# First row group of a four-way recurrent convolution: rows placed within SBUF, x on two queues, first weights placed by PE, coefficient chain in PSUM

## The chip, the cores and the metric

The kernel runs on one core of one Trainium2 chip. The metric is the device time of one launch in microseconds (us). Everything is float32. In the profile PE is the matrix engine, PEld its weight loads, DVE the vector engine, ACT the scalar engine, POOL the GpSimd engine, and SP the engine that does nothing but issue DMAs; ACT and POOL issue some too. L741 is line 741 of the kernel before.

## The reference

The input x has 32 images of 48 channels, 64 rows (H) and 128 columns (W). Two layers each do x = x + conv(gn(x)); every layer has its own weights.

```python
def _gn(v, G=16, eps=1e-5):            # mean and variance per image and group of 3 channels
    g = v.reshape(B_, G, C_ // G, H_, W_)
    return ((g - mean(g)) / sqrt(var(g) + eps)).reshape(v.shape)

def step(w, b):                        # one step of a scan over rows or columns
    def f(carry, inp):
        nxt = inp + _conv1d(carry, w, b)     # 48 to 48 channels, 5 taps, along the other axis
        return (nxt, nxt)
    return f
# conv: scan down over the 64 rows, up again (same weights), right over the 128 columns, left again
x = x + _L0_conv_ref(_gn(x), ...)
x = x + _L1_conv_ref(_gn(x), ...)
```

Each scan is a chain: a row needs the row before it. All rows of an image must be read before its mean and variance, hence the scale and offset of its first row, are known.

## The kernel before, in words

The images form four groups of 8. `PHASES` lists twelve phases: a "rows" phase does the down and up scans of one group (2 x 63 steps), a "cols" phase the right and left scans of two groups (2 x 127 steps). Phase 0 is rows of group 0 in layer 0; phase 1 is rows of group 1. A step is 9 products on PE of 128x128 float32 (18 matmuls in the trace, L741) into three PSUM tiles, and three adds on DVE (L750) that put bias and input row on top. The step's matmuls of the next row wait for these adds.

For the products, a row lies as 384 values (8 column residues e = w mod 8, times 48 channels) over 3 blocks of 128 partitions (`PIECES`, ten runs of partitions, says where each (e, channel range) lies), and 16 column blocks x 8 images in the free dimension. Three slots of the SBUF tile `arena` hold half an image group's rows each; a fourth part of it is `stage`. The order of the work is written by hand: `at(t, fn)` puts a piece of work ahead of step t, and `in_order` fixes, engine by engine, the order in which the program gives the instructions. An engine that waits therefore holds back everything behind it.

What precedes phase 0 is `first_group`:

- x of group 0 comes by 16 DMAs on SP (`take_in`, one per image and half), with channel and half of the rows interleaved over 96 partitions. `parts[i]` holds one half. DVE takes statistics of each image (`bn_stats`, L422).
- The weights of the first scan go from DRAM to a DRAM scratch (`taps`), and from there by 25 small DMAs to their places; ten more bring the biases. All of these are on ACT's queue.
- Rows 0 to 7 come into step layout by products with 0/1 matrices on PE (`rows_by_product`, L1074) and copies from PSUM on ACT (L1081).
- All 64 rows are permuted by copies of POOL and ACT (`permute`, L569, four copies of 96x256 for a pair of rows) and written to DRAM (`put_out`, tensor `xin`); rows 8 to 63 come back from there in step layout (`move_rows`, ten DMAs for eight rows, in runs of 128 bytes). The copy in DRAM also serves the residual, later.
- `scaling` turns statistics into scale and offset: products with a mask on PE average over channel groups, and DVE and ACT form 1/sqrt(var + eps) with one Newton step (L354 to L401).
- The rows are scaled in place: rows 0 to 3 by DVE (`scale_at_once`, L625), rows 4 to 47 by ACT (`scale_rows`, L614), rows 48 to 63 by POOL (`scale_at_once` again).

Group 1's input is prepared during phase 0 by `plan_input`: loads into `nats1` (which lies where the second half of group 0's x lay), permuting on POOL, `put_out`, statistics on ACT (L443, L435), and `scaling` on DVE between the steps (L460, L465, L470 and on).

Of the kernel before, what the change touches and what calls it, by code (L numbers as in the profile page):

```python
# [120 lines left out]
def kernel(  # L121
# [49 lines left out]
    early = const([FULL, 3 * WEIGHTS + NG * N + BN], "early")  # L171
# [5 lines left out]
    wt["left"] = const([FULL, NG, NG * FULL], "wleft")  # L177
# [7 lines left out]
    junk = early[:, 3 * WEIGHTS + NG * N :]  # L185
# [34 lines left out]
    def lines(t, h0, h1):  # L220

        t = t.rearrange("c (i q a n) -> a c i q n", i=E8, q=NQ, a=NH)[h0 // E8]
        return t[:, h0 % E8 : h0 % E8 + h1 - h0].rearrange("c i q n -> c (i q) n")
# [53 lines left out]
    def sided(t):  # L277

        return t.rearrange("(c s) n -> s c n", s=2)

    def load_constants(dma):
        for s in range(2):
            dma(sided(mask_sb)[s], mask[SIDES[s], SIDES[0]])
        for e, c0, c1, o, p0 in PIECES:
            dma(bd[p0 : p0 + c1 - c0, o], bias[c0:c1])
# [5 lines left out]
    def spread_masks():  # L291
        for s in range(2):
            nc.gpsimd.tensor_copy(mask_x.rearrange("p (c s) -> p s c", s=2)[:, s], mask_sb)
        for e, c0, c1, o, p0 in PIECES:
            nc.gpsimd.tensor_copy(maskp[:, o, p0 : p0 + c1 - c0], mask_sb[:, c0:c1])

    def spread_row_masks():
        for s in range(2):
            nc.gpsimd.tensor_scalar(
                mask_r.rearrange("p o (c s) -> p o s c", s=2)[:, :, s],  # L300
# [10 lines left out]
    def scaling(key, layer, g, averages, masks, slack=0):  # L311
# [5 lines left out]
        pool = nc.gpsimd if slack else nc.vector  # L317
# [25 lines left out]
        mean = small("mean")  # L343
        spare = small("dev")
        dev = spare[0 : FULL if n > 1 else PX, 0:n]
        if n > 1:
# [3 lines left out]
            expand(ps[:, 1 : 1 + NG], mean_c)  # L350
            yield
            nc.vector.tensor_tensor(dev, mean_p, ps[:, 1 : 1 + NG], ALU.subtract)
        else:
            nc.vector.tensor_tensor(dev, mean_p, ps[0:PX, 0:1], ALU.subtract)  # L354
        if n > 1:
            nc.vector.tensor_copy(mean, ps[:, 1 : 1 + NG])
# [6 lines left out]
        if n == 1:  # L363
            expand(ps[:, 2 + NG :], dev[:, 0])
        else:
# [5 lines left out]
            expand(ps[:, 2 + NG :], var_c)  # L371
        yield
        var = small("var")
        nc.vector.tensor_scalar(var, ps[:, 2 + NG :], GN_EPS, None, ALU.add)

        std = small("std")
        nc.scalar.activation(std, var, AF.Sqrt)
        if n == 1:
            expand(ps[:, 1 : 1 + NG], mean_p[:, 0])
        yield  # L380
        if n == 1:
            nc.vector.tensor_copy(mean, ps[:, 1 : 1 + NG])
        yield
        for _ in range(slack):
# [4 lines left out]
        pool.tensor_tensor(t0, var, r0, ALU.mult)  # L389
# [3 lines left out]
        scale, offset = (  # L393
            stat_pool.tile(
                [FULL, NG, GB], F32, tag=f"{t}{layer}{g}", name=f"{t}{layer}{g}"
            )
            for t in ("scale", "offset")
        )
        pool.tensor_tensor(scale, r0, t0, ALU.mult)
        pool.tensor_tensor(offset, mean, scale, ALU.mult)  # L400
        pool.tensor_scalar(offset, offset, -1.0, None, ALU.mult)  # L401
        coeffs[layer, g] = scale, offset
# [150 lines left out]
    def take_in(g, r0, nat, batches=slice(0, GB)):  # L553


        n = nat.shape[-1] // W
        src = x[g * GB : (g + 1) * GB].rearrange("b c (s h) w -> (c s) b (h w)", s=2)
        dma(nat[:, batches], src[:, batches, r0 * W : (r0 + n) * W])
# [12 lines left out]
    def put_out(g, r, perm):  # L571


        n = perm.shape[-1] // (W * GB)
        for s in range(2):
            h = s * HALF + r
            dma(
                lines(source[0][g], h, h + n),
                sided(perm)[s].rearrange("p (m n) -> p m n", n=LINE),
            )  # L580
# [37 lines left out]
    def scale_at_once(k, h0, h1, eng):  # L618

        _, layer, g = PHASES[k]  # L620
        view = row_views(k)[h0 // HALF][:, :, h0 % HALF : h0 % HALF + h1 - h0]
        view = view.rearrange("p o h (k b) -> p o (h k) b", b=GB)
        for t, op in zip(coeffs[layer, g], (ALU.mult, ALU.add)):
# [585 lines left out]
```

## Time and profile before

| what | value |
|---|---|
| runs shown, median (lowest to highest) | 4286.53 us (4279.23 to 4295.52), 3 runs |
| profiled execution: time / span | 4290.3 us / 4288.2 us |
| PE busy, share of the span | 4058.9 us, 95% |
| DVE / ACT / POOL busy | 2164.5 / 1340.1 / 886.2 us |
| mean granted PE clock | 0.981 |
| DMA | 680.12 MB in 2116733 packets, 2005440 of them under 512 bytes |

The page gives busy times of the engines, and a map of the span in 40 slices. A timeline row reads: start in us, length in us, engine, line, operation, output tile <- input tiles, shapes, count, and in brackets the idle time before it and what ended it. A row of the waits reads: who waited for whom, us in total, times, longest. A row of windows gives for each engine the busy time and the number of instructions, then the granted clock, the busy share of the 16 DMA engines and GB/s. An answer on a tile gives for a kind of instruction the least, median and greatest duration in ns; for a DMA that is the time of its issue.

### The profile page before, as it was taken

Reading aid. Unit: us, or ns where it says so; the run is one execution under the profiler, and the core shown is the slowest. Engines: PE = TensorE matmul, PEld = TensorE weight load, DVE = VectorE, ACT = ScalarE, POOL = GpSimd, SP = SyncE. Lnnn points to the kernel's source line nnn. Section 1 sums busy time; section 2 is a strip of 40 time slices with the busy share of each in tenths; the row PEclk is TensorE's granted clock in tenths of the full one; section 3 lists DMA queues with packets and bytes.
Section 4 is the critical chain, followed back from the end, with each engine's and each line's share of the span. In section 5 each row is a group of like instructions: output and inputs, shape, how many; then the busy total and the mean of one; then the engine's idle time right before and its main releaser. Section 6 shows DMA issues by size and latency. Waiting matters only on the chain. (4 is left out here: it accounts for less than half of the span.)

```text
span 4288.2 us, 89979 instructions
## 1 busy us (share of the span) xinstructions
PE 4058.9 (95%) x36648; PEld 4029.3 (94%) x36648; DVE 2164.5 (50%) x6503; ACT 1340.1 (31%) x2662; POOL 886.2 (21%) x906
## 2 busy tenths in 40 slices
PE   3699998999999999998999999999999999999992
PEld 1699998999999999998999999999999999999992
DVE  6345444446664444444446654444444444444443
ACT  1584301435793564100006772613000002210122
POOL 4271001325323020010005310000000024510352
PEclk9899999999999999999999999999999999999996
DMA  9599799857998979679308979939289049999999
GB/s 213 113 216 162 105 167 168 245 127 213 230 198 156 163 140 160 103 127 206 85 1 242 222 154 149 148 50 161 43 140 200 1 78 247 247 243 156 180 202 182
DMA packets 2116733, 680.12 MB, mean 159 GB/s; under 512 B 2005440, under 2 KB 2056160, under 8 KB 2076384
## 3 DMA queue, kind: packets, MB, share of 16 engines
q1 hardware_dynamic: 2015904, 581.64, 70.2%
q10 hardware_dynamic: 97216, 86.44, 9.9%
q0 software_dynamic: 3200, 6.30, 0.5%
q8 instruction: 288, 4.72, 0.5%
q14 instruction: 125, 1.02, 0.1%
HBM read 397.38 MB, written 295.98 MB: 162 GB/s over the span
## 5 line engine op out<-in xcount | busy, mean ns | idle before, releaser
L614 ACT ACTIVATE arena<-arena,offset,scale 128x256 f32<-128x256 f32 (+2 forms) x816 | 575.6, 801 | 432.9 <-DMA arena<-mid 176.1
L673 POOL TENSOR_TENSOR arena<-arena 128x2048 f32<-128x2048 f32 x80 | 363.1, 4553 | 1386.0 <-PE step_10l L741 434.1
L569 POOL COPY arena<-arena 96x256 f32<-96x256 f32 x448 | 265.0, 650 | 553.8 <-DMA arena<-in_x 444.2
L512 ACT ACTIVATE early<-arena 128x256 f32<-128x256 f32 x192 | 129.4, 674 | 477.2 <-POOL arena L673 471.2
L741 PE MATMUL step_00r<-arena,early 128*128 128x128 f32 x2286 | 251.5, 274 | 14.1 <-DMA arena<-upa 14.1
L741 PEld LDWEIGHTS step_00r<-arena,early 128*128 128x128 f32 x2286 | 251.1, 185 | 14.5 <-issue 14.4
L741 PE MATMUL step_01r<-arena,early 128*128 128x128 f32 x2286 | 250.6, 273 | 14.4 <-DMA arena<-upa 14.4
L741 PEld LDWEIGHTS step_01r<-arena,early 128*128 128x128 f32 x2286 | 250.4, 185 | 14.6 <-issue 14.5
L741 PE MATMUL step_11r<-arena,early 128*128 128x128 f32 x2286 | 251.3, 273 | 8.2 <-DVE arena L750 8.2
L741 PEld LDWEIGHTS step_11r<-arena,early 128*128 128x128 f32 x2286 | 250.8, 185 | 8.7 <-DVE arena L750 8.6
L741 PE MATMUL step_00l<-arena,wleft 128*128 128x128 f32 x2286 | 249.1, 272 | 0.0
L741 PEld LDWEIGHTS step_00l<-arena,wleft 128*128 128x128 f32 x2286 | 248.6, 184 | 0.0
L741 PE MATMUL step_10l<-arena,wleft 128*128 128x128 f32 x2286 | 248.5, 272 | 0.0
L741 PE MATMUL step_11l<-arena,wleft 128*128 128x128 f32 x2286 | 248.5, 272 | 0.0
L741 PE MATMUL step_01l<-arena,wleft 128*128 128x128 f32 x2286 | 248.4, 272 | 0.0
L741 PE MATMUL step_10r<-arena,early 128*128 128x128 f32 x2286 | 248.4, 272 | 0.0
L741 PEld LDWEIGHTS step_10l<-arena,wleft 128*128 128x128 f32 x2286 | 248.4, 184 | 0.0
L741 PEld LDWEIGHTS step_11l<-arena,wleft 128*128 128x128 f32 x2286 | 248.4, 184 | 0.0
L741 PEld LDWEIGHTS step_01l<-arena,wleft 128*128 128x128 f32 x2286 | 248.4, 184 | 0.0
L741 PEld LDWEIGHTS step_10r<-arena,early 128*128 128x128 f32 x2286 | 248.4, 184 | 0.0
L698 ACT COPY arena<-arena 128x256 f32<-128x256 f32 x172 | 99.7, 656 | 411.5 <-POOL arena L673 162.2
L240 ACT COPY early<-arena 128x1 f32<-128x1 f32 x2 | 0.4, 191 | 657.9 <-DVE arena L750 657.9
(189 smaller groups left out, 7171.3 us busy)
## 6 DMA issues: line engine op xcount, KB each, us to landing
arena<-in_x SPq DMA_DIRECT2D x24, 1536.0 KB, 11.6
xin<-arena SPq DMA_DIRECT2D x96, 384.0 KB, 4.7
arena<-xin SPq DMA_DIRECT2D x96, 384.0 KB, 8.5
mid<-arena SPq DMA_DIRECT2D x96, 384.0 KB, 7.8
arena<-mid SPq DMA_DIRECT2D x192, 192.0 KB, 4.2
upb<-arena SPq DMA_DIRECT2D x192, 192.0 KB, 3.9
arena<-upb SPq DMA_DIRECT2D x96, 384.0 KB, 12.3
arena<-xin SPq DMA_DIRECT2D x186, 192.0 KB, 4.3
```

The source lines that it names most:

```text
L240: fn(*args)
L512: nc.scalar.activation(junk[:, 0:n], view[:, b], AF.Identity, accum_out=self.sum[:, i, j : j + 1])
L569: copy(dst[:, r, q], src[:, r0 + r, q])
L614: nc.scalar.activation(args[0], args[0], AF.Identity, bias=args[2], scale=args[1])
L673: eng.tensor_tensor(unit, unit, nat, ALU.add)
L698: copy(by_w(perm)[:, a], src[:, a])
L741: nc.tensor.matmul(part(whole(ps[o])[0:m], -s), weights[:, i, at : at + m], part(src(i), s), start=seen[o] == 1, stop=seen[o] == left[o],)
```

## The change

Layout: the two row sides of an image now lie in partitions 0 to 47 and 48 to 95 (before they alternated), so a load or store of both sides is two DMAs where it was one. The `left` weights join the tile `early`, where three weights' places lie free at first and serve as a ring buffer for four row copies.

First group: x comes in pairs of images, one side on POOL's queue and the other on ACT's. `parts[0]` now holds rows 0 to 31, `parts[1]` rows 32 to 63. Weights, biases and masks are loaded compactly on SP and placed by products of PE with 0/1 matrices, copied out by ACT. ACT's table for sqrt is loaded first. `four` copies four rows of each side into a buffer (a row as one copy of 96x1024) and 20 DMAs on SP place them from there straight into the step layout, in runs of 512 bytes; three buffers are used (`spot`, `ring`, `room`). `spot` lies where images 6 and 7 of `parts[1]` go, so these are loaded after it was read. The copies for DRAM (`to_cols`) follow apart, on POOL. Rows 0 to 3 are scaled by 24 operations of DVE (`scale_first`), all others by ACT.

Coefficients: in the chain without slack (groups 0, 1 and 3) intermediate values stay in PSUM, so no DVE operation has two operands in SBUF. Group 1's preparation is put 6 steps later, and its loads 22.

```diff
@@ scaling
+        if not slack:
+            far = ps[0:PX, 1 + NG : 2 + NG]
+            nc.vector.tensor_tensor(far, mean_p, ps[0:PX, 0:1], ALU.subtract)
+            nc.vector.tensor_tensor(dev, mean_p, ps[0:PX, 0:1], ALU.subtract)
+            nc.vector.tensor_tensor(far, far, dev, ALU.mult)
+            nc.vector.tensor_tensor(dev, far, var_p, ALU.add)
+            yield
+            expand(var, dev[:, 0])
+            yield
+            nc.vector.tensor_scalar(var, var, GN_EPS, None, ALU.add)
+            r0 = small("std")
+            nc.scalar.activation(r0, var, AF.Sqrt)
+            expand(mean, mean_p[:, 0])
+            yield
+            yield
+            nc.vector.reciprocal(r0, r0)
+            nc.vector.tensor_tensor(var, var, r0, ALU.mult)
+            nc.vector.tensor_tensor(var, var, r0, ALU.mult)
+            nc.vector.tensor_scalar(var, var, -0.5, 1.5, ALU.mult, ALU.add)
+            nc.vector.tensor_tensor(scale, var, r0, ALU.mult)
+            nc.vector.tensor_tensor(offset, mean, scale, ALU.mult)
+            nc.vector.tensor_scalar(offset, offset, -1.0, None, ALU.mult)
+            return
...
@@ take_in
-        src = x[g * GB : (g + 1) * GB].rearrange("b c (s h) w -> (c s) b (h w)", s=2)
-        dma(nat[:, batches], src[:, batches, r0 * W : (r0 + n) * W])
+        src = x[g * GB : (g + 1) * GB].rearrange("b c (s h) w -> s c b (h w)", s=2)
+        for s in range(2):
+            dma(nat[s * C : (s + 1) * C], src[s, :, :, r0 * W : (r0 + n) * W])
...
-    plan_input(1, [starts[0] + 46 + 6 * j for j in range(8)], 5, 1, nats1, tiles[2:4])
+    plan_input(1, [starts[0] + 52 + 6 * j for j in range(8)], 5, 1, nats1, tiles[2:4])
...
@@ first_group
+        ring = early[:, WEIGHTS : WEIGHTS + 4 * n]
+        spot = arena[:, 3 * SLOT + 2 * UNIT :]
+        room = arena[:, 2 * SLOT : 2 * SLOT + 4 * n]
...
+        def load(i, b0, b1, *sides):
+            for s in sides:
+                queue = nc.scalar if s else nc.gpsimd
+                dma(parts[i][s * C : (s + 1) * C, b0:b1], src[i, s, :, b0:b1], queue)
...
+        def place_rows(i, r0, n, perm):
+            src = perm[0:PX].rearrange("(s c) (r e m) -> s e c r m", s=2, r=n, e=E8)
+            dst = row_views(0)[i].rearrange("p o (s h) m -> s o p h m", s=2)
+            for s in range(2):
+                for e, c0, c1, o, p0 in PIECES:
+                    dma(dst[s, o, p0 : p0 + c1 - c0, r0 : r0 + n], src[s, e, c0:c1])
...
+        load(0, 0, 2, 0, 1)
+        load_kernel()
+        load_masks()
+        nc.vector.memset(junk[:, 0:1], 0.0)
+        nc.scalar.activation(junk[:, 0:1], junk[:, 0:1], AF.Sqrt)
+        make_select()
+        for b in range(2, 8, 2):
+            load(0, b, b + 2, 0, 1)
+        load(1, 0, 2, 0, 1)
+        load(1, 2, 4, 0)
+        load(1, 4, 6, 0)
+        place_kernel()
+        spread_masks()
         for b in range(GB):
             stats.take(0, parts[0], b)
...
+        pool, act = nc.gpsimd, nc.scalar
+        four(0, 0, spot, pool, pool, act, act)
+        to_four(0, 4, ring, pool, pool, act, act)
+        load(1, 2, 4, 1)
+        place_rows(0, 4, 4, ring)
+        load(1, 4, 6, 1)
+        load(1, 6, 7, 0, 1)
+        load(1, 7, 8, 0, 1)
+        four(0, 8, ring, pool, pool, act, act)
+        four(0, 12, ring, pool, pool, pool, pool)
         for b in range(GB):
             stats.take(NBN // 2, parts[1], b)
             stats.aggregate(b)
...
         for _ in scaling("x0", 0, 0, stats, x_masks):
             pass
...
+        scale_first(0, 4)
         scale_rows(0, 4, 8)
...
+        for h in range(8, HALF, 8):
+            scale_rows(0, h, h + 8)
+        blocks = [ring[:, j * n : (j + 1) * n] for j in range(4)]
+        for r in range(rows):
+            to_cols(0, r, blocks[r % 4])
+        for r in range(0, rows, 4):
+            four(1, r, (room, ring)[r // 4 % 2], pool, pool, pool, pool)
+        scale_rows(0, 32, 36)
+        scale_rows(0, 36, 40)
+        for h in range(40, H, 8):
+            scale_rows(0, h, h + 8)
+        for r in range(rows):
+            to_cols(1, r, blocks[r % 4])
         take_in(1, 0, nats1[0])
...
     for j in range(1, 4):
-        at(starts[0] + 22 + j, take_in, 1, 4 * j, nats1[j])
-    at(starts[0] + 26, scale_at_once, 0, 48, 56, nc.gpsimd)
-    at(starts[0] + 33, scale_at_once, 0, 56, 64, nc.gpsimd)
+        at(starts[0] + 44 + j, take_in, 1, 4 * j, nats1[j])
```

## The prediction

> **What bounds the kernel now.** I read the page first: PE is busy for 4058.9 of the 4288.2 us of the span, so what this change can move is time in which PE stands. The waits of PE over the first 260 us show where it stands early, and the timeline of PE shows when.
>
> ```profile
> PE rows L1074 <- DMA arena<-in_x: 41.7, 1, 41.7
> PE step_00d L741 <- DVE arena L750: 31.7, 6, 14.9
> PE step_00d L741 <- DVE arena L625: 24.7, 1, 24.7
> ```
> ```profile
> 107.83 17.66 PE L741 MATMUL step_00d<-arena,early 128*128 128x128 f32 x144 [24.72 <-DVE arena L625]
> ...
> 175.60 0.79 PE L741 MATMUL step_00d<-arena,early 128*128 128x128 f32 x2 [13.62 <-DVE arena L750]
> ...
> 208.63 0.80 PE L741 MATMUL step_00d<-arena,early 128*128 128x128 f32 x2 [14.85 <-DVE arena L750]
> 209.60 63.38 PE L741 MATMUL step_00d<-arena,early 128*128 128x128 f32 x556 [0.17 <-DVE arena L750]
> 272.81 73.28 PE L741 MATMUL step_00u<-arena,early 128*128 128x128 f32 x666
> ```
>
> The first scan starts at 107.83, stands three times (2.5, 13.6 and 14.9 us, at rows 8, 24 and 32, whose scaled values are not there), and turns upward at 272.81. A step is 18 matmuls; 666 in 73.28 us make 1.98 us a step. Sixty-three steps without a stand need 125 us, so 272.8 - 125 = 148 us is all that lies ahead of the turn besides PE's work.
>
> The timelines of DVE and POOL tell why the start is so late:
>
> ```profile
> 78.61 0.16 DVE L354 TENSOR_TENSOR dev_x<-mv_x_x,ps_x 96x8 f32<-96x8 f32 x1 [9.43 <-PE ps_x L322]
> ...
> 83.58 22.07 DVE L389 TENSOR_TENSOR dev_x<-var_x,std_x 128x24 f32<-128x24 f32 x1
> 105.68 0.18 DVE L390 TENSOR_TENSOR dev_x<-dev_x,std_x 128x24 f32<-128x24 f32 x1
> ```
> ```profile
> 100.96 4.64 POOL L569 COPY early<-arena 96x256 f32<-96x256 f32 x8
> ```
>
> A 0.18 us operation took 22.07 us and ended 0.05 us after POOL's row of copies (100.96 + 4.64 = 105.60). Before it, 9.43 us went in waiting for PE, which was still moving rows with its products.
>
> How x arrives and what an issue costs is in the windows and in SP's answer on the arena:
>
> ```profile
> 5.00:30.00 25.00, 0.00 (x0) 0.00 (x0) 12.34 (x20) 0.00 (x0) 0.00 (x0) 1.00 0.66 162
> 42.50:62.50 20.00, 20.00 (x23) 6.82 (x22) 17.92 (x32) 7.07 (x14) 9.21 (x25) 1.00 1.02 259
> ```
> ```profile
> L231 SPq DMA_DIRECT2D xin<-arena x26: 554/568/691, 44.7 to 91.7; - x26
> L231 SPq DMA_DIRECT2D arena<-xin x20: 312/823/1457, 74.1 to 103.2; - x20
> L231 SPq DMA_DIRECT2D arena<-in_x x16: 312/412/836, 0.7 to 42.2; - x16
> ```
>
> The last two numbers of a window are the DMA share and GB/s: 162 GB/s while the weights' small loads are mixed in, 259 GB/s with the 16 engines full.
>
> **The change, part by part.** *Coefficients.* L389 has its first operand in PSUM now: its 22.07 us go. So do the 9.43 us behind PE's products, which are dropped. The 24 scalings that `scale_first` adds on DVE I price at the 0.19 us of small DVE operations: 4.6 us; the upper bound is that they wait as L389 did, which is a rival below. The Trainium skill (SBUF — State Buffer, "Who interferes with whom") says that a DVE instruction with two SBUF inputs contends with GpSimd reads, as in L389's row, but also that tensor_scalar can enter a two-port mode and contend; by that rule the 24 would be held up to POOL's next pause.
>
> *Weights by PE.* The 25 placing DMAs and 10 bias DMAs (ACT's queue until 36.6 us) become 6 loads on SP and 38 matmuls. Bounds per matmul: 0.24 us (128x8) and 0.93 us (18 of 512 columns in 16.71 us), so 9 to 35 us; the pieces are mostly under 200 columns, so some 11 us from about 10 us on. That ends at 21, ahead of the rows on ACT, which come after the copies of the result: nothing. At the upper bound ACT's first rows would be 18 us late.
>
> *x on two queues.* x is 12.6 MB: 49 us at 259 GB/s. The first image took 5.6 us for 3.0 us of transfer, so 2.6 us of overhead, and part 0 (6.3 MB) lands at 24.3 + 2.6 = 27 us, not 44. One queue alone reached these 259 GB/s, so what two queues gain here is only the time that stalled issues cost up to 40 us. Against the second queue stands the Trainium skill, DMA: Bandwidth & Descriptors ("Rules for kernel authors"): spreading DMAs over issuing engines brings no bandwidth, as they share the same 16 engines; by that rule part 0 would land no sooner than at full rate, the same 27 us.
>
> *Rows SBUF to SBUF.* This is the new path. Before, 56 rows came back from DRAM in 128-byte runs and 8 by PE's products. Now all 64 are copied in 32 pairs by POOL and ACT, and each four copies (a set) are placed by 20 DMAs on SP. A shape between the rows above costs 0.41 to 0.57 us to issue; I take 0.50, so 10 us for a set, plus 2.5 to land. For 512-byte runs the engines stay below that: 1024-byte runs moved at 378 GB/s (43 ns on one engine), 128-byte runs at 158 GB/s (13 ns); 240 runs on each engine are 3 to 10 us. A row copy: 4 of 593 ns were 2.37 us; a 48-element one took 161 ns, so one of 1024 is about 2.2 us. POOL then also copies all 32 row pairs for DRAM, 16 copies = 38 us for each half.
>
> Order on the queues, each step from the one before:
> - 27: part 0 is in. 32: rows 0 to 3 copied.
> - 55: set 0 landed. Small transfers beside x wait their turn (a 36 KB one took 5.2 us beside x, a 192 KB one 3.1 us alone), so I add x's next six images (4.7 MB, 18 us) and the set's 10 us rather than overlap them.
> - The last two images lie where set 0's copies stand, so they are requested only now, from ACT and POOL, and land at 64; set 1 lands at 71. Sets 2 and 3 reuse one buffer, so POOL and ACT wait for landings; ACT's sqrt stands behind its two copies of set 2.
> - 76: copies of set 2, then sqrt. 78: coefficients. 83: first step, 25 us earlier than 107.83.
> - 88: set 2 landed; 97: set 3 copied on POOL; 109: landed; 12.3 us of scaling (24 of 128x128 on ACT): 122. Row 8 was due at 99, so PE stands 23 us.
> - 147: POOL's 38 us of copies for DRAM, which must finish before rows 32 on may overwrite part 0. 156: next set copied, 168 landed, 178 scaled; row 32 was due at 169: 9 us.
> - The last three sets are bound by SP and buffers: 178, 190, 200. Scaling rows 40 to 47 ends at 212, and row 63 at 212 + 23 x 1.98 = 258: the turn is 14 us earlier. (Row 40 was due at 194, so that stand is 18 us.) After a long stand the granted clock fell, to 0.50 in the window 200 to 210, and 32 matmuls came in the next 5 us in place of 48, so 1.7 us are lost; before has two such stands, the forecast three, which I leave within the rounding.
>
> *Group 1 gives most of that back.* Its loads need part 1 consumed: 200 + 38 = 238. The first landed 10 us after issue (225.3 to 235.3), so ACT's statistics start at 248 and need the 104.5 us they took (235.29 to 339.8): 352. DVE's first operation on the second pass (L470) came at 344.4 and phase 1's first matmul at 400.8, 56.4 later; the schedule now puts this 6 steps (11.9 us) later, leaving 44.5. So phase 1 starts no sooner than 352 + 44.5 = 397 against 400.8. DVE waits there in order, with the steps' adds behind it, so PE stands for about 10 us.
>
> The sum: -4 us. The profiled execution took 4290.3 us (span 4288.2), 3.8 over the median of 4286.5; 4290.3 - 4 - 3.8 = 4282.5, say 4283. Later groups' loads split in two halves cost one more issue (0.4 to 0.6 us) each on SP, in phases where PE does not wait for them; if that cover were gone, 24 x 0.5 = 12 us. The other edits only move buffers.
>
> **Rivals.** *Faster, the sets cost less.* At 0.41 us an issue eight sets on the path save 8 x 20 x 0.09 = 14 us, copies at 1.7 us another 7, set 0 hidden beside x up to 10: 31 us less, 4252. For it: 0.41 is a measured row. Against: that row has one run for each partition. If the sets were off the path altogether, the turn would come at 83 + 125 = 208: 4218; but POOL's 58 copies and the buffer reuse speak against it.
>
> *Slower, SP's queue.* The rows that SP wrote into the same pieces of partitions took 0.823 us (median). At that price the eight sets cost 8 x 20 x 0.32 = 51 us more: 4334. It decides from about 0.65 us an issue (25 us more). For it: the same ten pieces; against: those had 1536 runs of 128 bytes, these 192.
>
> *The wait is not removed but moved.* If the 24 scalings wait for POOL as L389 did, the first step comes at POOL's next pause, 97 to 100. Row 8 is held until 122 anyway, so anything up to 105 is free: 4283 again.
>
> **How the numbers follow.** Forecast 0.46, moved wait 0.06, cheaper sets 0.21, sets off the path 0.05, SP's queue 0.22. About 0.5% (21 us) is what a measurement of this kernel can tell from no change: faster 0.26, same 0.52, slower 0.22. The range takes the low bound of issue and copies (-25: 4258) and 0.64 us an issue (+22: 4305), a little wider for x's rate: 4256 to 4308.
>
> **What would show it.** Right: first step near 83; L389's successor under 0.3 us; PE standing some 20 us at row 8 for ACT's scaling, again at 32 and 40; POOL's last copies of part 1 near 238; DVE waiting for ACT near step 100. Wrong: sets landing within 8 us of their copies, or the first group-1 load before 225 or after 255; an issue over 0.65 us on SP; PE at row 8 without a stand.

## The result, and the profile after

The changed kernel took 4335.35 us (median of 5 runs, 4331.10 to 4337.65); the kernel before, timed beside it, 4294.39 (5 runs, 4279.23 to 4309.93). The ratio is 1.0098, with a 95% interval of 1.0069 to 1.0126: about 1% slower, where 4283 within 4256 to 4308 had been forecast. The profiled execution of after took 4331.1 us with a span of 4329.3, 41.1 us more than the span of before.

The first table sets the starts of PE's scans (the first matmul of each in the timeline) beside the forecast; the turn of a phase is the start of its upward scan. From the turn of phase 1 on, every scan of after starts 40 to 45 us later than that of before, to the end: all of the loss is made in the first 570 us.

| us | before | forecast | after |
|---|---|---|---|
| first step | 107.8 | 83 | 92.6 |
| turn of phase 0 | 272.8 | 258 | 279.1 |
| first load of group 1 issued | 225.3 | 238 | 263.5 |
| phase 1 starts | 400.8 | 397 | 429.1 |
| turn of phase 1 | 526.6 | | 567.6 |

The timeline of PE after (start, busy us, engine, line, operation, number; in brackets the idle time before and what ended it) shows the stands that the change leaves and those that it makes:

```profile
92.58 0.79 PE L767 MATMUL step_00d<-arena,early 128*128 128x128 f32 x2 [3.49 <-DVE arena L644]
...
130.80 0.80 PE L767 MATMUL step_00d<-arena,early 128*128 128x128 f32 x2 [15.51 <-DVE arena L776]
...
188.00 9.95 PE L767 MATMUL step_00d<-arena,early 128*128 128x128 f32 x72 [6.36 <-DVE arena L776]
201.06 0.49 PE L767 MATMUL step_00d<-arena,early 128*128 128x128 f32 x2 [3.11 <-DVE arena L776]
...
230.51 0.80 PE L767 MATMUL step_00d<-arena,early 128*128 128x128 f32 x2 [19.21 <-DVE arena L776]
...
376.47 4.17 PE L767 MATMUL step_00u<-arena,early 128*128 128x128 f32 x18 [16.24 <-DVE arena L776]
...
470.60 0.77 PE L767 MATMUL step_01d<-arena,early 128*128 128x128 f32 x2 [9.65 <-issue]
```

Rows 8, 32, 36 and 40 of phase 0 come late (15.5, 6.4, 3.1 and 19.2 us); in the upward scan DVE waits in order for ACT's statistics of group 1 (16.2 us); and phase 1 stands at its row 16 (9.7 us). The last one is new and was in no step of the forecast. It costs a little more than its length: from 470 to 480 PE's granted clock was 0.59 and PE made 48 matmuls, where the kernel before, which has no stand there, made 94 at 1.00.

The timeline of SP's queue after names what fills the way. `arena<-arena` and `arena<-early` x20 are sets, `xin<-early` the copies for DRAM, `arena<-in_x` the loads of group 1:

```profile
44.32 21.47 SPq L233 DMA_DIRECT2D arena<-arena  x20
65.96 59.05 SPq L233 DMA_DIRECT2D arena<-early  x60
...
170.59 13.88 SPq L233 DMA_DIRECT2D arena<-arena  x20
184.57 13.73 SPq L233 DMA_DIRECT2D arena<-early  x20
198.41 13.26 SPq L233 DMA_DIRECT2D arena<-arena  x20
211.76 12.94 SPq L233 DMA_DIRECT2D arena<-early  x20
227.41 35.96 SPq L233 DMA_DIRECT2D xin<-early  x32
263.47 15.84 SPq L233 DMA_DIRECT2D arena<-in_x  x8
```

In the kernel before, the loads of group 1 go out 38 us earlier:

```profile
225.30 8.60 SPq L231 DMA_DIRECT2D arena<-in_x  x4
```

Each set of part 1 costs SP 13 to 14 us, with the next one close behind, and the queue's answer by operand gives the issue (min/median/max ns):

```profile
L233 SPq DMA_DIRECT2D arena<-early x100: 582/605/1904, 66.0 to 224.1; - x100
...
L233 SPq DMA_DIRECT2D arena<-arena x60: 582/605/2074, 44.3 to 211.1; - x60
```

With what lies between two issues a set of part 1 takes 12.9 to 13.9 us, so 0.65 to 0.69 us a DMA, not 0.50. POOL's timeline shows the other half of the chain: it stands for landings (59 us of the 64 between 39.8 and 103.4: 20.0 before it requests the last two images, 23.0 and 15.8), then copies part 0 for DRAM (36.4 us), the four sets of part 1, and part 1 for DRAM (36.4 us), one behind the other:

```profile
83.79 3.85 POOL L1114 COPY early<-arena 96x1024 f32<-96x1024 f32 x2 [22.96 <-DMA arena<-early]
103.43 7.70 POOL L1114 COPY early<-arena 96x1024 f32<-96x1024 f32 x4 [15.80 <-DMA arena<-early]
...
126.50 36.40 POOL L591 COPY early<-arena 96x256 f32<-96x256 f32 x62 [2.27 <-DMA arena<-early]
162.75 7.81 POOL L1114 COPY arena<-arena 96x1024 f32<-96x1024 f32 x4
...
226.18 36.38 POOL L591 COPY early<-arena 96x256 f32<-96x256 f32 x62 [2.34 <-DMA arena<-early]
```

Only at 262.6 is part 1 consumed and group 1's first load issued. That is the place where the time went; the experiments show that it sets the rest.

### The profile page after: what moved, and what is told of

Read it like the earlier page. It is cut to its first block, busy times and chain, and to the rows that moved or that the text cites. A ratio compares the mean times of both kernels' runs of the same rounds, so it can differ in the third digit from the quotient of the medians.

```text
span 4329.3 us, 90368 instructions
## 1 busy us (share of the span) xinstructions
PE 4053.7 (94%) x36684; PEld 4043.5 (93%) x36684; DVE 2142.2 (49%) x6524; ACT 1376.2 (32%) x2726; POOL 924.3 (21%) x950
## 5 line engine op out<-in xcount | busy, mean ns | idle before, releaser
L591 POOL COPY arena<-arena 96x256 f32<-96x256 f32 x384 | 227.4, 646 | 535.3 <-DMA arena<-in_x 270.8
L767 PE MATMUL step_00l<-arena,early 128*128 128x128 f32 x2286 | 249.1, 272 | 0.0
L767 PE MATMUL step_01l<-arena,early 128*128 128x128 f32 x2286 | 248.7, 272 | 0.1
L767 PEld LDWEIGHTS step_01l<-arena,early 128*128 128x128 f32 x2286 | 248.4, 184 | 0.3 <-DVE arena L776 0.3
L767 PEld LDWEIGHTS step_00l<-arena,early 128*128 128x128 f32 x2286 | 248.6, 184 | 0.0
L767 PE MATMUL step_10l<-arena,early 128*128 128x128 f32 x2286 | 248.5, 272 | 0.0
L767 PE MATMUL step_11l<-arena,early 128*128 128x128 f32 x2286 | 248.5, 272 | 0.0
L767 PEld LDWEIGHTS step_10l<-arena,early 128*128 128x128 f32 x2286 | 248.4, 184 | 0.0
L767 PEld LDWEIGHTS step_11l<-arena,early 128*128 128x128 f32 x2286 | 248.4, 184 | 0.0
L465 ACT ACTIVATE early<-arena 96x512 f32<-96x512 f32 x192 | 121.4, 632 | 278.5 <-DMA arena<-in_x 212.8
```

The costliest lines, as they stand in the source:

```text
L465: nc.scalar.activation(junk[0:PX], piece, AF.Identity, accum_out=self.sum[:, at[0], at[1]],)
L591: copy(dst[:, r, q], src[:, r0 + r, q])
L767: nc.tensor.matmul(part(whole(ps[o])[0:m], -s), weights[:, i, at : at + m], part(src(i), s), start=seen[o] == 1, stop=seen[o] == left[o],)
```

## Experiments

Medians are of all runs of a kernel; 4335 is the changed kernel, and every ratio is to the kernel before.

**1. The coefficients' chain alone.** The kernel before with the change's `scaling()` and nothing else: the chain of group 0 is on DVE as it was, but its intermediate values are kept in `ps`, in PSUM.

> The kernel before with one part of the change: the chain of the first coefficients on DVE, values in PSUM. Theory (what decides is when part 1 is copied out and group 1's statistics can start; the first step's time is worth nothing): the 22.07 us operation falls to 0.2 us, the first step comes at about 86 instead of 107.8, the turn at 262 to 272, phase 1 still starts at 398 to 402, and the time is that of before within 6 us. Rival (the wait at the chain was on the path): all of it stays, some 20 us faster than before.

Measured: 4294.49 us, ratio 1.0006 (0.9992 to 1.002): no change. But the first step came at 106.7, not at 86. DVE's timeline of this run shows why:

```profile
81.35 0.30 DVE L368 RECIPROCAL std_x<-std_x 128x24 f32<-128x24 f32 x1 [0.26 <-ACT std_x L364]
82.85 0.19 DVE L369 TENSOR_TENSOR ps_x<-ps_x,std_x 128x24 f32<-128x24 f32 x1 [1.20 <-PE ps_x L333]
...
83.96 21.65 DVE L374 TENSOR_SCALAR offset<-offset 128x24 f32<-128x24 f32 x1
105.53 0.55 DVE L647 TENSOR_TENSOR arena<-arena,scale 128x384 f32<-128x384 f32 x1
```
```profile
100.93 4.64 POOL L591 COPY early<-arena 96x256 f32<-96x256 f32 x8
```

The product with an operand in PSUM takes 0.19 us, as the forecast had it, and the next operation with SBUF on both sides takes 21.65 us and ends at 105.61, within 0.1 us of the end of POOL's run of copies (100.93 + 4.64 = 105.57). The stall was moved by five instructions. Not every operation from SBUF to SBUF is held: the reciprocal L368 took 0.30 us beside the same copies, as long as in the changed kernel. In the changed kernel L374 took 0.18 us and the 24 scalings 6.00 us (0.25 each, 0.19 forecast), while POOL stood, from 87.6 to 103.4. Since the first step hardly moved here, this run says nothing on what an earlier first step is worth. Experiment 7 does: its first step comes 20 us later than the changed kernel's and its turn 18 us earlier. The Trainium skill (SBUF — State Buffer, "Who interferes with whom") says that tensor_scalar can take a two-port mode and then excludes GpSimd, and so the reverse; this run agrees, with 21.65 us.

**2. Half of ACT's statistics of group 1**, the gate that the forecast put before phase 1. The kernel leaves out the other half of each run.

```
+            self.width = BN // 2 if key == "x1" else BN
...
-                        piece = nat[:, b, n * BN : (n + 1) * BN]
+                        piece = nat[:, b, n * BN : n * BN + self.width]
```

> The changed kernel, where ACT's statistics of group 1 read only the first half of each run of 512 elements (the other half is left out of them). Theory: ACT's stretch of 105 us falls to about 66 and ends near 343 instead of 382; the stands of 16.2 and 2.2 us in the upward pass go, phase 1 starts at about 405 instead of 429 (it is then bound by the turn at 279 and 63 steps of 1.98 us), and the time falls by about 24 us, to 4311; the stand of 9.7 us in phase 1, if it comes from POOL's and SP's copies of group 1, stays or grows. Rival (phase 1 is late for another reason, such as rows that come back late from DRAM): no change, 4335 within 5 us.

Measured: 4334.37 us. The statistics ended at 365 instead of 382 and phase 1 started 14.8 us earlier, and nothing was gained, since row 16 then stood longer (PE's timeline of this run):

```profile
414.25 31.86 PE L768 MATMUL step_01d<-arena,early 128*128 128x128 f32 x288
471.58 0.77 PE L768 MATMUL step_01d<-arena,early 128*128 128x128 f32 x2 [25.47 <-issue]
```

The theory fell in this form. Rows 16 to 31 of group 1 come back from DRAM by SP's reads, from 433 to 454 in this run and the changed kernel alike; they follow from loading, copying and writing group 1's rows. The lines are of before and of after:

```profile
392.25 19.99 SPq L231 DMA_DIRECT2D arena<-xin  x20
```
```profile
432.82 19.80 SPq L233 DMA_DIRECT2D arena<-xin  x20
```

These reads go out 40.6 us later, as the turn is 41.0 later.

**3. Half of part 1's placing DMAs on ACT's queue.** ACT's scalings of rows 32 to 39 move in between the sets with it.

```
-            place_rows(i, r0, 4, perm)
+            place_rows(i, r0, 4, perm, (None, nc.scalar if i else None))
...
-        scale_rows(0, 32, 36)
-        scale_rows(0, 36, 40)
+            if r in (4, 8):
+                scale_rows(0, 28 + r, 32 + r)
```

> The changed kernel, where the ten placing DMAs of the second side of each set of part 1 are issued by ACT instead of SP. Theory (issue on one queue is what a set costs): a set of part 1 is bound by POOL's four copies (7.8 us) instead of 13.3 us of issue, so the last copies of part 1 end 13 to 20 us earlier (near 245 instead of 262.5), group 1's statistics and phase 1's start move by as much, and the time is 4315 to 4322. Rival (engines or landing bound, not issue): sets stay 13 us apart and the time stays within 5 us of 4335.

Measured: 4322.97 us (1.0046 to 1.0095). SP's stretch for the four sets went from 54 us (170.6 to 224.7) to 35 us (174.6 to 209.5), part 1's copies ended 9 us earlier, and the turn of phase 1 came 9.3 us earlier; 13 to 20 us had been expected of the copies. Issue on one queue is part of the price of a set; the buffers and landings behind it kept the rest.

**4. Twice the DMAs, the same bytes.**

```
-                    dma(dst[s, o, p0 : p0 + c1 - c0, r0 : r0 + n], src[s, e, c0:c1])
+                    for r in range(0, n, 4 >> i):
+                        rr = slice(r, r + (4 >> i))
+                        dma(
+                            dst[s, o, p0 : p0 + c1 - c0, r0 + r : r0 + r + (4 >> i)],
+                            src[s, e, c0:c1, rr],
+                        )
```

> The changed kernel, where each set of part 1 is placed by 40 DMAs of two rows instead of 20 of four; the bytes are the same. Theory (issue bound): 80 more issues, at 0.5 to 0.65 us, lie on the path: phase 1 starts 40 to 52 us later (470 to 480) and the time is 4375 to 4387. Rival (bytes or copies bound): less than 10 us more.

Measured: 4386.74 us, 51 more. Eighty more issues delayed group 1's first load by 52.1 us, which is 0.65 us each, and phase 1's start by 52.4. A set's price is its number of issues. SP's queue of this run, the last two sets and the load:

```profile
225.80 25.78 SPq L233 DMA_DIRECT2D arena<-arena  x40
251.68 25.83 SPq L233 DMA_DIRECT2D arena<-early  x40
...
315.57 14.68 SPq L233 DMA_DIRECT2D arena<-in_x  x8
```

**5. Other blocks for the last copies of part 1.**

```
+        blocks = [room[:, j * n : (j + 1) * n] for j in range(4)] + blocks
-            to_cols(1, r, blocks[r % 4])
+            to_cols(1, r, blocks[r % 8])
```

> The changed kernel, where the last copies of part 1 for DRAM begin in the four blocks of the buffer that is free one set earlier. (After the statistics were halved without effect on the time, the theory is: what decides is when group 1's rows have been loaded, copied and sent to DRAM, and that follows the end of part 1's copies one for one.) Theory: POOL no longer stands at 221 for the landing of the last set; its copies end some 13 us earlier, near 249, and the time falls by 11 to 14 us, to 4321 to 4324. Rival (SP's order or the landing of group 1's loads decides): within 4 us of 4335.

Measured: 4327.14 us. The copies began 13.1 us earlier, at 208.0, but stood four times for landings of both buffers (1.3 to 2.4 us) and ended at 253.5, 9.1 us earlier; the turn of phase 1 came 12.0 us earlier. The time is 3 us above what was expected (4321 to 4324).

**6. The weights copied out of PSUM later.**

> The changed kernel, where ACT copies PE's placed weights out of PSUM after its rows of the first two sets and not before. Theory: ACT's rows start at about 32 instead of 40.4, set 0 is issued at 36 instead of 44, lands 6 to 8 us earlier, and all that follows from it (last two images, set 1, coefficients, part 1's copies) moves by as much: 4327 to 4330. Rival (sets beside x's transfers are bound by x and not by their start): set 0 lands within 3 us of 70.6 and the time stays at 4335.

Measured: 4328.78 us. Set 0 was issued at 36.8 instead of 44.3, but its 20 DMAs took 24.7 us instead of 21.5, it landed at 67.9 instead of 70.6, set 2 was copied only 2.5 us earlier and the first load of group 1 issued 2.7 us earlier. So the expected time was met, but not by the theory: set 0 landed as the rival had it, 14.8 us behind the sixth image of x's second half, against 14.7 in the changed kernel. Of the 12 us by which rows 0 to 3 missed the forecast, some 3 count up to the load: the rest is absorbed by x's transfers. The turn of phase 1 came 7.1 us earlier and the time fell by 6.6; what made the 4 us behind the load is not shown.

**7. Part 0's copies for DRAM in POOL's idle stretch**, into rows 8 to 15 and 24 to 31 of the first slot, written by ACT's queue.

```
         load(1, 4, 6, 1)
+        for r in range(8):
+            to_cols(0, r, free[r % 6], nc.scalar)
         load(1, 6, 7, 0, 1)
         load(1, 7, 8, 0, 1)
+        for r in range(8, 16):
+            to_cols(0, r, free[r % 6], nc.scalar)
...
-        for r in range(rows):
-            to_cols(0, r, blocks[r % 4])
```

> The changed kernel, where POOL makes its 16 copies of part 0 for DRAM in the stretch from 40 to 84 us in which it stands, into rows of the first slot that are still free, and ACT's queue writes them. Theory: 38 us of POOL's work leave the path: set 4 is copied at about 111 to 125 instead of 162.75, the stands at rows 32 to 40 (28.7 us) go, part 1's copies end near 215 to 225 and the time is 4295 to 4305. Rival (the 6.3 MB beside x and beside the first sets, or DVE's chain standing for POOL's copies, cost as much as they free): the first sets and images come 15 us later or more and the time is above 4320.

Measured: 4305.38 us, ratio 1.0023 (1.0013 to 1.0032): 30 of the 41 us came back. The load of group 1 was issued at 238.5, the stands at rows 32 to 40 were gone and the turn of phase 0 came at 260.7. Part of the rival was true too: ACT's row copies stood behind its writes until 103, and the first step came at 112.3 instead of 92.6, for which PE paid nothing that lasts.

**8. All of these at once**, with the second halves of group 1's first loads on ACT's queue.

> All of these together: half of part 1's placing DMAs on ACT's queue, late copies of the weights, part 0's copies for DRAM early, other blocks for part 1's, and the second halves of group 1's first loads on ACT's queue. Theory: the savings add up as far as the end of part 1's copies goes (some 70 us, to about 190), until the turn and the 63 steps behind it set phase 1's start: 4250 to 4280, faster than both kernels. Rival (each hides behind the same next wait): 4300 or more.

Measured: 4312.52 us, slower than experiment 7 alone and over 30 us above what was expected. ACT executes in order, and its share of part 1's DMAs stood behind the scaling of rows 8 to 31: SP issued its half of the first set of part 1 from 142.0, ACT from 166.6, and POOL stood 24.2 us for that landing. A queue is free only if its engine is.

**9. Second halves of group 1's loads on ACT's queue, alone.**

> The changed kernel, where the second halves (partitions 48 to 95) of group 1's first four loads are issued by ACT's queue, beside the first halves on SP. Theory: loads of 48 partitions one behind the other on one queue move 160 GB/s (6.3 MB from 263.5 to 302.7) where 96 partitions moved 203 GB/s before the change (225.3 to 256.3); on two queues the halves run together, the four pairs have landed 8 us or more earlier, group 1's statistics start some 3 us earlier and POOL's second copy is no longer held until 305, so that the time falls by 5 to 9 us, to 4328. Rival (bytes bound): last landing within 3 us of 302.7, 4335.

Measured: 4328.67 us, the expected number, but by luck and not by the mechanism: ACT's halves landed at 258.7 to 282.3, SP's then at 287.0 to 303.5, and the last landing was where it had been (302.7). The turn of phase 1 came 1.6 us later; the difference in the total arose after 3744 us, where the edit has no part. The Trainium skill (DMA: Bandwidth & Descriptors, "Rules for kernel authors") advises against splitting a transfer into partition halves, since both go through the same 16 engines. The last landing is in line with this but is no test of it: SP's halves, of partitions 0 to 47, went out only at 274.3 (263.5 in the changed kernel) and landed 4.9 to 5.8 us apart, ACT's 3.8 and 4.3, and experiment 16 finds that side slow when it moves alone.

**10 and 11. Group 1's rows written by POOL's queue**, alone, and with half statistics. The write stays at its place of the written-out order. Only the call is shown.

```
...
-                at(t + i * work / per + 4, put_out, g, rows * j + r, HALF, perm)
+                at(t + i * work / per + 4, put_out, g, rows * j + r, HALF, perm, nc.gpsimd if g == 1 else None)
```

> The changed kernel, where the 64 DMAs that write group 1's rows to DRAM are issued by POOL's queue, behind the copies that they belong to, instead of by SP. Theory (two gates stand one behind the other: ACT's statistics of group 1 set phase 1's first step, and the way of group 1's rows through POOL, SP and DRAM sets its row 16): POOL no longer stands 18 us for writes that are queued behind SP's reads, the stand of 9.7 us at row 16 of phase 1 goes, phase 1 still starts near 429, and the time falls by 8 to 10 us, to 4326. Rival (the reads of rows 16 to 31 are late because of SP's own 40 writes and reads before them): the stand stays, 4335.

> The two edits together: group 1's statistics over half of each run (the other half is left out of them), and group 1's rows written by POOL's queue. Theory of the two gates: halving the statistics alone changed nothing since row 16 then waited 25.5 us; with both, phase 1 starts at 404 to 414 and has no stand at row 16, so that the time falls by 23 to 27 us, to 4308 to 4312. Rival (a third wait of the same length stands behind them): 4326 or more.

Measured: 4395.59 and 4392.94 us, 60 and 58 slower, with whole and half statistics alike. POOL's timeline of the first:

```profile
434.44 4.72 POOL L591 COPY arena<-arena 96x256 f32<-96x256 f32 x8 [6.02 <-issue]
439.11 1.26 POOL L233 DMA_DIRECT2D xin<-arena  x2
445.19 4.68 POOL L591 COPY arena<-arena 96x256 f32<-96x256 f32 x8 [4.83 <-DMA xin<-arena]
449.82 1.26 POOL L233 DMA_DIRECT2D xin<-arena  x2
```

In POOL's order a copy comes ahead of the other buffer's write, and it waits for a landing; the write that is ready stands behind it. The 16 blocks took 194 us (278.9 to 473.2) instead of 142. Both expectations missed this. What it shows is that the way of group 1's rows sets phase 1, with either length of the statistics.

**12. Several at once** (part 0's copies early for 12 rows, POOL's writes as in 10, halves on ACT).

> The changed kernel with 12 of POOL's 16 copies of part 0 made in the stretch in which it stands (6 before the last two images are requested, 6 after), group 1's rows written by POOL's queue, and the second halves of its first loads on ACT's queue. Theory: the end of part 1's copies moves from 262.5 to about 235, the two gates of phase 1 open 30 to 35 us earlier: phase 1 starts at 390 to 400 and does not stand at row 16: 4280 to 4295, the same as before the change or slightly faster. Rival (the copies' writes on ACT's queue hold up its rows, the coefficients and set 2 by as much): 4300 or more.

Measured: 4376.73 us. It carries the fault of experiment 10, so it shows nothing about its other parts.

**13 and 14. The same writes, each directly behind its copy**, alone and with half statistics.

```
...
-                at(t + i * work / per + 4, put_out, g, rows * j + r, HALF, perm)
+                at(t + i * work / per + (0 if g == 1 else 4), put_out, g, rows * j + r, HALF, perm, nc.gpsimd if g == 1 else None)
```

> The changed kernel, where POOL's queue writes group 1's rows, each write directly behind its copy. (With the writes in the old places of the order POOL stood before the next copy with the other buffer's write still unissued, and the time grew by 60 us: the way of group 1's rows does set phase 1.) Theory of the two gates: POOL's 16 blocks take 110 to 120 us instead of 142, row 16 of phase 1 is there in time, phase 1 starts at 425 to 430 as ACT's statistics allow, and the time falls by 8 to 10 us, to 4326. Rival (writes from POOL's queue land too slowly beside the loads): as slow as or slower than 4335.

> The same, with ACT's statistics of group 1 over half of each run (the other half is left out of them). Theory: neither gate is left, phase 1 starts at 405 to 414 without a stand at row 16, and the time falls by 20 to 27 us, to 4308 to 4315, where halving the statistics alone had given nothing. Rival (the way of the rows is still last): within 4 us of the kernel of the run before, which has whole statistics.

Measured: 4328.70 and 4327.02 us. In the first the blocks took 116 us and the stand at row 16 fell from 9.65 to 1.65 us, as expected. The turn of phase 1 came 11.4 us earlier, of which 3.6 were left when the first scan of layer 1 began (1467.4): waits of the later phases shift the distance between two kernels by some microseconds, so the turn tells more of an early edit than the total. In the second the expected 20 us did not come: phase 1 stood 4.2 us at its first rows and 6.3 at row 16. SP's reads of rows 0 to 15 took 38.2 us there (369.4 to 407.7), against 22.8 in the changed kernel: they follow the rows' way too. So whole statistics and the rows' way are two gates of nearly the same length, both hung on group 1's first load.

**15. Experiments 7 and 13 together.**

> The kernel with POOL's 16 copies of part 0 made early (4305 us), and group 1's rows written by POOL's queue directly behind their copies. Theory: its stand of 9.95 us at row 16 of phase 1 goes, phase 1 starts at 400 as before: 4294 to 4298, no slower than the kernel before the change. Rival: the stand stays, 4305.

Measured: 4300.10 us, ratio 1.0007 (0.9997 to 1.0016): the time of before, 2 us above what was expected.

**16. The sides of x exchanged between the two queues.**

> The changed kernel with the two queues of x exchanged: ACT's queue carries partitions 0 to 47, POOL's 48 to 95. After the change POOL's transfers alone (38 to 49 us) take 940 to 975 ns for 8 KB, some 140 GB/s, and 505 ns while both queues run. If it lies with the half of the partitions (a transfer of 48 partitions reaches half of the engines' rate), POOL's transfers alone stay at 940 to 975 ns with the other half; if it lies with the side 0 to 47, they fall to about 505 ns. No change of the time over 5 us either way.

Measured: one run, 4339.88 us. The windows give, at the end of each line, the DMA share and GB/s: first of after, then of this run.

```profile
12.00:32.00 20.00, 11.07 (x40) 9.83 (x40) 14.55 (x25) 0.55 (x2) 1.94 (x12) 1.00 1.03 253
36.00:44.00 8.00, 3.92 (x19) 3.83 (x18) 6.10 (x12) 4.04 (x4) 3.84 (x3) 1.00 1.03 140
49.00:53.00 4.00, 0.00 (x0) 0.00 (x0) 0.41 (x1) 0.00 (x0) 0.00 (x0) 1.00 1.01 239
```
```profile
20.00:40.00 20.00, 16.22 (x62) 14.39 (x61) 12.49 (x21) 1.09 (x4) 4.49 (x14) 1.00 1.00 206
44.00:50.00 6.00, 0.00 (x0) 0.00 (x0) 5.16 (x9) 6.00 (x4) 2.00 (x3) 1.00 1.04 143
52.00:56.00 4.00, 0.00 (x0) 0.00 (x0) 0.00 (x0) 0.00 (x0) 0.00 (x0) 1.00 0.97 224
```

The first line of each has both queues. In the second only partitions 0 to 47 have transfers left, by POOL's queue in after and mostly by ACT's here: 140 and 143 GB/s with the engines full. In the third only 48 to 95, by the other queue, with the first small transfers of set 0 beside them: 239 and 224. So the slow rate goes with the side and not with the queue, and not with half of the partitions as such. The forecast's 259 GB/s does not hold while only the first side has work; that part 1's first side is requested ahead of its second (images 2 to 5 at 6.2 and 6.7 us on POOL's queue, at 40.4 and 40.7 on ACT's, behind the copies of the weights) leaves 12 us of the slow one.

**17 and 18. A version faster than both.** Part 0's copies early, POOL's writes behind their copies, the other blocks and the late weights together; in the second, SP instead of ACT writes part 0's rows 8 to 15.

> The changed kernel with part 0's copies made early, group 1's rows written by POOL's queue directly behind their copies, the other blocks for part 1's copies, and the weights copied late. Theory: in the runs so far the upward pass of phase 1 began 300 to 304 us after the first load of group 1 was issued, 293 with POOL's writes; the load comes here at 226 to 232 (238 with the early copies alone), so that the pass begins at 519 to 525, against 526.6 in the kernel before: 4287 to 4294, faster than before by 0.1 to 0.2%. Rival (with the loads this early, the statistics and the turn at 258 set phase 1's start instead): 4297 to 4302, the same as before.

> The same, but the second half of part 0's early writes is issued by SP instead of ACT. Theory: ACT's rows of set 2 and its square root no longer stand behind eight rows' writes (until 103 us), the first step comes 6 to 8 us earlier and set 2 some 4 us: as the kernel of the run before, or up to 4 us faster. Rival (SP's sets then stand behind the writes): 4 us or more slower.

Measured: 4285.64 us, ratio 0.9981 (0.9968 to 0.9994), and 4281.37 us, ratio 0.9972 (0.9961 to 0.9983): faster than before by 0.2 and 0.3%, little, but with both intervals below 1. PE's timeline of the second has one stand of phase 0 left and none of phase 1:

```profile
142.09 0.80 PE L767 MATMUL step_00d<-arena,early 128*128 128x128 f32 x2 [18.30 <-DVE arena L776]
143.06 110.90 PE L767 MATMUL step_00d<-arena,early 128*128 128x128 f32 x988 [0.17 <-DVE arena L776]
253.79 81.14 PE L767 MATMUL step_00u<-arena,early 128*128 128x128 f32 x738
...
388.00 124.73 PE L767 MATMUL step_01d<-arena,early 128*128 128x128 f32 x1134
```

Set against each other, the runs say one thing. The distance from the issue of group 1's first load to the turn of phase 1 is nearly a constant:

| kernel | load issued | turn of phase 1 | distance |
|---|---|---|---|
| before | 225.3 | 526.6 | 301.3 |
| chain alone | 223.5 | 524.5 | 301.1 |
| early copies of part 0 | 238.5 | 540.2 | 301.6 |
| other blocks | 254.4 | 555.6 | 301.2 |
| half on ACT's queue | 254.5 | 558.3 | 303.8 |
| late weights | 260.8 | 560.5 | 299.7 |
| **after** | 263.5 | 567.6 | 304.2 |
| half statistics | 265.0 | 568.3 | 303.4 |
| twice the DMAs | 315.6 | 615.4 | 299.8 |
| POOL's writes behind the copies | 263.6 | 556.3 | 292.6 |
| version 17 | 226.8 | 519.6 | 292.8 |
| version 18 | 221.3 | 512.6 | 291.2 |

The load is issued when part 1 has been copied out. First steps between 90 and 112 us leave no mark on the last column. The distance is no constant of its own: it is the way of group 1's rows. Where POOL's order holds that way up (experiments 10 and 11) it is 364 and 363 us. Experiments 14 (half statistics), 15 and 16 have 296.5, 294.4 and 299.2; in 8, 9 and 12 two queues issue the load at different times, so one distance does not describe them.

## Why the prediction was wrong, step by step

The step that failed is the time at which part 1 is consumed and group 1's first load can go out: 238 forecast, 263.5 measured, past the 255 that the prediction itself named as a sign of being wrong. Two terms ahead of it were too small, and behind it a second wait was missing.

**Right.** L389's successor, L369, is 0.19 us. That an earlier first step is worth little by itself: it came 15.2 us earlier than before and the turn 6.3 us later. The order of PE's stands (rows 8, 32 and 40: 23, 9 and 18 us forecast; 15.5, 6.4 with 3.1 more at row 36, and 19.2 measured) and the chain of POOL's copies, sets and landings. POOL's pair copy is 1.93 to 1.95 us (2.2 taken), its 16 copies for DRAM 36.4 plus their stands (38 taken). ACT's statistics took 104.9 us (104.5), DVE's wait for them near step 100 held PE for 16.2 and 2.2 us (about 10 taken), and phase 1 started 47 us behind them (44.5 taken).

**The term that failed: a set's issue.** "I take 0.50, so 10 us for a set": 0.605 at the median and 0.65 with the gap, some 13.4 us for a set. The last three sets, which SP bounds, were taken as 10 to 12 us apart (168, 178, 190, 200) and were issued 13.3 to 14.0 apart, the last landing at 226. The forecast's bounds of 0.41 and 0.57 came from rows with other shapes, and the rival "SP's queue" was said to decide from 0.65 us an issue: only with the gap is that reached. That its time, 4334, was met is luck: its reckoning had 0.82 us an issue and no other loss. The forecast also counted 192 runs for each of the 20 DMAs of a set and so 240 on each of the 16 engines; only 12 have 192, four have 128 and four 64, which makes 192 an engine. Nothing hung on it, for the issue takes the same 0.60 to 0.61 us with all three.

**The term that failed: x and what stands beside it.** Part 0 was forecast in at 27 and was in at 31.9; rows 0 to 3 were copied at 44.3 (32), set 0 landed at 70.6 (55). The placing on PE was to end at 21 and ended at 39.9: the last small loads of weights and the biases landed only at 18.2 and 21.7 beside x, not at 10, the last 70 of its matmuls in the trace then ran for 18.18 us, where 11 had been taken for all, and ACT's rows came behind the copies of the result. Taking these copies out of the way brought the load forward by some 3 us (experiment 6). The larger part is x itself: for 12 us (36 to 48) it moved at 141 GB/s, not 259. Its next six images were in at 55.9, where 27 + 18 = 45 had been taken; set 0 landed 14.7 us behind them instead of 10, and the last image at 77.1 instead of 64.

**The steps between.** These two make the gap up to the load: set 3 landed at 126.4 (109), part 0's copies ended at 162.9 (147), part 1's at 262.6 (238). So 15 to 17 us come from the time up to set 3 and another 9 from the sets of part 1, and every one of them delays group 1. In the second stretch the four sets lost 12 us, and the copies, cheaper than taken, gave 3 back.

**The step that was not there.** The forecast let phase 1 wait for ACT's statistics alone, 352 + 44.5 = 397. With its own late load (277.1 instead of 248 landed: 25.5 us from the issue, 3.6 from the way in) that rule gives 426, near the measured 429. But halving the statistics gained nothing (experiment 2): the way of group 1's rows through POOL, SP and DRAM is a second gate of the same length, and it adds the stand of 9.65 us at row 16. From 429.1 - 400.8 = 28.3 us at the start of phase 1 the loss grows to 41.0 at its turn, by this stand and the slower steps behind it. The forecast priced the split loads at one issue each; the eight halves took SP 15.8 us instead of 8.6 for four, and their landings 39.2 us (263.5 to 302.7) instead of 31.0.

**The other rivals.** "Moved wait": true of the edit alone (experiment 1), absent in the whole change, where POOL stands when DVE's chain runs. "Sets cost less" had only the pair copies for it (1.93 us against 2.2 taken), "sets off the path" nothing.

## What to carry to other kernels

When work at the start of a kernel feeds a buffer that the next stage's input is loaded into, price the change by the time at which that buffer is free again, not by the first step: here twelve kernels with first steps from 90 to 112 us turned phase 1 between 291 and 304 us after that load, and two whose rows were held up on POOL at 363. Take the price of a DMA issue from a row of the same shape, and where none exists carry the far bound through every set on the path. Before taking one gate away, look for a second one of the same length behind it, and before moving a DMA to another queue, read what its engine has queued ahead of it.

## What the runs showed of the hardware

- A DVE tensor_scalar from SBUF to SBUF (experiment 1) and a tensor_tensor with both operands in SBUF (before) waited to the end of POOL's run of copies (21.65 and 22.07 us for operations of 0.18 us), while one with an operand in PSUM took 0.19 us and a reciprocal from SBUF to SBUF 0.30, beside the same copies.
- An SBUF to SBUF DMA of 64, 128 or 192 runs of 512 bytes costs SP 0.60 to 0.61 us at the median, whichever of the three, and twice the DMAs with half the runs cost the same each (25.8 us for 40, 0.65 us a DMA with the gap).
- Small loads issued beside 8 KB runs come late: the last of the weights, issued at 2.6 us, had landed at 18.2, the biases, issued at 3.1, at 21.7, the masks, issued at 3.6 and 6.6, at 25.1 and 29.4.
- Partitions 0 to 47 of x alone moved at 140 and 143 GB/s (952 and 938 ns at the median for 8 KB) on either queue, partitions 48 to 95 alone at 239 and 224 (541 and 551 ns). Whether the partitions or the DRAM addresses that go with them make it stays open.
